# Moving work within a graph-and-expert kernel: loads, routing, one-hots and last steps in another order

## The chip, the cores and the metric

The kernel runs on one core of a Trainium2 chip. Its time is the device time of one execution in microseconds (us). The kernel before was run 9 times: median 2648.38 us, from 2645.98 to 2657.72. One execution was profiled.

## What is computed

A network of two layers over 3125 nodes with 256 features and 50000 edges, all in fp32. Each layer adds a graph convolution and a feed-forward part, each on a layer-normed input. The reference, cut (`seg_sum` and `seg_max` run over the edges of one target node `dst`):

```python
# layer 0: relational sums, 16 relations; then a mixture of 16 experts, 2 per node
h = layernorm(x)
x = x + seg_sum((h @ W_rel[r])[edge_type, src] * edge_weight, dst)
h = layernorm(x);  p = top2(softmax(h @ gate_w + gate_b))        # renormalized
x = x + sum_e p_e * ((silu(h @ w1[e]) * (h @ w2[e])) @ w3[e])
# layer 1: two graph attention convolutions of 8 heads; then shared MLP + 4 experts, 2 per node
def gat(h, W, a_src, a_dst, b):
    h = (h @ W).reshape(N, 8, 32)
    e = leaky_relu((h*a_src).sum(-1)[src] + (h*a_dst).sum(-1)[dst], 0.2)
    z = exp(e - seg_max(e, dst)[dst])
    return seg_sum(h[src] * (z / seg_sum(z, dst)[dst]), dst) + b
x = x + gat(elu(gat(layernorm(x), W1, ...)), W2, ...)
h = layernorm(x)
x = x + mlp3(h) + sum_e softmax(top2(softmax(h @ gW + gb)))_e * expert3_e(h)
```

The edges come sorted by target node.

## The kernel before

The nodes are cut into T = 25 tiles of R = 125. On PE, DVE, ACT and SP the instructions stand in the order in which the Python code issues them (`manual_schedule`), except for SP in the first stage, where a scheduler places the DMAs; POOL issues the indirect DMAs (gathers and scatters) in the code's order. Buffers come from pools with a fixed number of copies (`bufs`), so that a writer waits for the readers of the copy before. The stages follow one another:

**Table stage (0 to 604 us).** For each tile, in two halves of eight relations, PE multiplies the layer-normed rows by all relational weights `w_rel` (L1259, `p_tr`), ACT copies the product (L1262, `tr`, two copies) and SP writes it to a table in DRAM (L1266, 1 MB). Beside that the edges are read, sorted into records and placed (`edge_records` after tile 2, `places` from tile 3, `sent` after tile 6). From tile 11 on (SA) the first half of the relational sums runs along: POOL gathers table rows of the edges (L111), PE multiplies them by one-hot rows `hot` and adds (L987, `half_summed`). `weights(l)` (L1214) loads the matrix of attention layer l (`wx`) and its vectors (`av`), and multiplies them; it is called behind tiles 19 and 21.

**Second half of the sums, and routing (604 to 958 us).** The loop over the 25 `items` (one tile of sums each, 10 gathers on POOL) has in each pass: the two halves of an item's sums, `fetch` (gathers) for the item two ahead, `hot` for the next, `turn` (transposed rows) and `logits` (expert scores) for earlier items. The items are two batches, 11 (TA) and 14. When all logits of a batch are there, `routing` (L1400), a generator of steps of mainly DVE and some PE, ACT and SP work, chooses two experts per node, counts, and finds each row's position among the experts' slots; then it scatters the batch's rows to `xs` (L1509, two scatters per tile on POOL: 22 and 28). The expert slots of the first batch (19) and the second (22) are cut into a list of steps, `pieces`; `take(slot_steps, n)` issues the next n of them. `turn_slot` (L1545 to L1551) loads a slot's rows.

**Expert slots (to 1372 us).** The rest of the steps, PE-bound; `back_beside` for the first batch's way back runs beside them: gather each node's two expert rows, add them (`add_back`, L1617), layer-norm (`centred`, `factors`, L1372 to L1383), transpose, multiply by `wx1` (`first_hidden`, L1623) and write the rows of the first attention table (`h_tab`, L1626); `in_parts` (L929 to L933) splits the target scores into three bf16 parts `ad`. `back_alone` does the same for the second batch when nothing else is left (1372 to 1444 us).

**Attention layers (1444 to 1982 and 2021 to 2554 us) and end.** `layer` goes over the tiles; in pass s the tile `new` is s + 1, `now` is s, `old` is s - 1. Per tile POOL gathers 17 x 128 rows of 264 columns (256 features and 8 scores) into `g` in three PARTS (6, 6 and 5). `scans` (L1771) makes running maxima over the edges, `carried` (L1797) takes them across partitions, with PE's transposes `p_c`; `scores` (L1810) gives `z`, `weighted` (L1841) the products of rows and z into a tile `m`, `summed` (L1848) the sums by the one-hot `oh` on PE (L1852), `means` the division. `one_hot` (L1794) and `destinations` (L1790) for the next tile stand at the end of a pass. After a tile of layer 1 come elu and the product with `wx2` (`tail1` to `tail4`), written to the second table. Layer 2 has the last feed-forward beside it: the tiles go in 13 `pairs` (the last holds one tile) through the steps `normalize`, `first_layers`, `gates`, `second_layers`, `choice`, `shares`, `spread`, `shared_out`, `third_layers`, `finish` (out by L2151). `run` gives each step when its lag is reached: pair k is due in pass 2k + 2 + lag. Seven extra passes (`more`) drain them.

Of the kernel before, what the change touches and what calls it, by code (L numbers as in the profile page):

```python
# [7 lines left out]
F32 = mybir.dt.float32  # L8
# [35 lines left out]
def gnn_kernel(ctx: ExitStack, tc: tile.TileContext, a: dict, out: bass.AP):  # L44
# [834 lines left out]
    def by_tiles(ctx, start_i, hard):  # L879
# [124 lines left out]
        with ExitStack() as mk:  # L1004
# [5 lines left out]
            for r0 in range(0, RELS, 8):  # L1010
                for k in range(2):
                    nc.sync.dma_start(w_rel[:, k, r0:r0 + 8], a["L0_gnn_weight"]
                                      [r0:r0 + 8, k * 128:(k + 1) * 128, :].rearrange("r p o -> p r o"))
                if r0 == 0:
                    load_x(1, 5)
# [198 lines left out]
            def weights(l):  # L1214

                wx = keep.tile([128, 2, D + 2 * H], F32, name=f"wx{l}")
                nc.sync.dma_start(wx[:, :, :D], a[f"L1_gnn_W{l}"].rearrange("(k p) o -> p k o", p=128))
                av = sb.tile([128, 2, 2], F32, name="av", bufs=2)
                for k, name in enumerate((f"L1_gnn_a_src{l}", f"L1_gnn_a_dst{l}")):
                    nc.sync.dma_start(av[:, :, k], a[name].rearrange("h c -> (h c)")  # L1220
                                      .rearrange("(m p) -> p m", p=128), allow_slow_non_contiguous=True)
                ab = sb.tile([128, 2, 2, H], F32, name="ab", bufs=2)
# [52 lines left out]
            wx = []  # L1275
            with tc.manual_schedule():
# [3 lines left out]
                for t in range(T):  # L1280
# [29 lines left out]
                    if t == 2:  # L1310
# [12 lines left out]
                    elif t in (19, 21):  # L1323
                        wx.append(weights(len(wx) + 1))
# [4 lines left out]
            wx1, wx2 = wx  # L1329
# [3 lines left out]
        with ExitStack() as st:  # L1333
# [286 lines left out]
            def first_hidden(w):  # L1620
# [6 lines left out]
                in_parts(pool, ad1[:, w.t], h[:, DX:])  # L1627
# [24 lines left out]
            def back_alone(b):  # L1652
                for w in b.items[:3]:
                    fetch_back(w)
                for k in range(b.n + 2):
# [5 lines left out]
                    if 0 < k <= b.n:  # L1661
                        factors(b, k - 1, k)
                        turn(b.items[k - 1], wk_ps.tile([128, 512], F32, name="sum", bufs=2))
                    if k > 1:
                        first_hidden(b.items[k - 2])
# [11 lines left out]
            with tc.manual_schedule(engines={ET.PE, ET.DVE, ET.Activation, ET.SP}):  # L1677
                slot_steps = pieces()
                route, routed = routing(batches[0]), None
                for s, w in enumerate(items):  # L1680
                    if 1 <= s < 12:
                        k, c = (0, 4 * (s - 1)) if s < 6 else (1, 4 * (s - 6))
                        blank(k, c, min(c + 4, USED[k]))
                    for k in range(2):
                        summed(w.r, k)
                        if s + 2 < T:
# [3 lines left out]
                        if s > 1 and k == 0:  # L1690
                            logits(items[s - 2])
                        if s and k == 1:
                            turn(items[s - 1], w.r.p)
                        if s > TA and routed is None and not take(route, 8):
                            routed = s
                            take(slot_steps, 1)
                        if routed is not None and s > routed + 2:
                            take(slot_steps, 2)
                    summed_up(w.r)
                    centred(w)  # L1700
                    if routed is not None and s == routed + 2:
                        take(slot_steps, 11)
# [3 lines left out]
                take(slot_steps, 2)  # L1706
                logits(items[-1])
                route = routing(batches[1])
                while take(route, 1):
# [13 lines left out]
        with ExitStack() as st:  # L1723
# [28 lines left out]

            def fetch(w):
                w.g = []
                for k, (i0, i1) in enumerate(PARTS):
                    g = pool.tile([128, i1 - i0, DX], F32, name=f"g{k}", bufs=2)
                    for i in range(i0, i1):
                        gather(g[:, i - i0, :], w.h_tab, src_i[:, w.t, i:i + 1])  # L1760
# [49 lines left out]
            def scores(w):  # L1810
# [13 lines left out]
                w.m = [pool.tile([128, i1 - i0, DX], F32, name=f"m{k}") for k, (i0, i1) in enumerate(PARTS)]  # L1824
                for m, (i0, i1) in zip(w.m, PARTS):
                    nc.scalar.copy(m[:, :, D:], w.z[:, i0:i1])  # L1826
# [14 lines left out]
            def weighted(w, k):  # L1841
                i0, i1 = PARTS[k]
                m, g = (v[k][:, :, :D].rearrange("q i (h c) -> q i h c", h=H) for v in (w.m, w.g))
                nc.vector.tensor_mul(m, g, w.z[:, i0:i1, :, None].to_broadcast([128, i1 - i0, H, HD]))  # L1844

            def summed(w, k):
# [4 lines left out]
                for i in range(i0, i1):  # L1851
                    nc.tensor.matmul(w.p, w.oh[:, i, :], w.m[k][:, i - i0, :], start=(i == 0), stop=(i == CT - 1))  # L1852
# [12 lines left out]
            def layer(h_tab, ad, bias, tail1, tail2, tail3, tail4, slot=None, end=None, more=0):  # L1865
# [348 lines left out]
```

## Time and profile before

The profiled execution took 2648.1 us, its span 2646.3 us, at a mean granted TensorE clock of 0.856.

| engine | busy us | share of the span | instructions |
|---|---|---|---|
| PE (matmul) | 1995.1 | 75% | 8600 |
| PE weight load | 1447.2 | 55% | 8600 |
| DVE | 1353.9 | 51% | 2859 |
| ACT | 809.3 | 31% | 1701 |
| POOL | 1389.1 | 52% | 1445 |

By stage (busy us): table 0 to 604: PE 500, DVE 283, POOL 223. Sums and routing 604 to 958: PE 240, POOL 263. Slots 958 to 1372: PE 392. Way back 1372 to 1444: PE 36, DVE 36. Attention layer 1: PE 323, DVE 362, POOL 405 of 538. Layer 2: PE 408, DVE 398, POOL 403 of 533. End 2554 to 2646: PE 71.

In the chain that ended last PE has 43%, POOL 16%, issue 13%, DMA 13% and DVE 9%. The shares are averages over stages; "issue" is time in which an engine waited for nothing that the profile shows, and POOL's gathers each have 0.30 us of it in front.

### The profile page before, as it was taken

The page shows a single profiled execution, that of the slowest core. Times are in us where ns is not written, and L with a number is a line of the kernel's source. Part 1 is how long each engine was busy: PE and PEld are TensorE (multiplying, and loading weights), DVE is VectorE, ACT ScalarE, POOL GpSimd, SP SyncE. Part 2 cuts the span into 40 slices and gives each one's busy share as a digit, 9 for nine tenths or more (in the row PEclk, how much of TensorE's full clock was granted, in tenths as well). Part 3 has the DMA queues.
Part 4 walks back from the last instruction along what each step waited for, and adds up shares of the span by engine and source line. Part 5 has one row for each costly group of instructions (what it writes and reads, how often), then busy time and mean ns, then how long its engine had stood idle before and what let it go on. Part 6 is the DMA issues. An engine that isn't in the chain of part 4 may idle for free.

```text
span 2646.3 us, 26683 instructions
## 1 busy us (share of the span) xinstructions
PE 1995.1 (75%) x8600; PEld 1447.2 (55%) x8600; DVE 1353.9 (51%) x2859; ACT 809.3 (31%) x1701; POOL 1389.1 (52%) x1445
## 2 busy tenths in 40 slices
PE   6788998795655999998974366666653687888887
PEld 2334455454444888886862254444542465666665
DVE  1358673223351432132115476767763677888872
ACT  2222222120111232242223333333331354555542
POOL 0100677446777724120024777777773777777740
PEclk9789999897777999998985677777876788999998
DMA  6532555443345757664533655555552554454520
GB/s 216 196 118 112 182 178 193 143 142 107 105 128 184 220 168 246 206 208 130 195 107 92 156 140 140 139 140 139 141 154 52 136 136 133 137 148 133 150 72 19
DMA packets 191857, 386.35 MB, mean 146 GB/s; under 512 B 39698, under 2 KB 112386, under 8 KB 185957
## 3 DMA queue, kind: packets, MB, share of 16 engines
q0 software_dynamic: 76464, 189.38, 27.6%
q1 hardware_dynamic: 104091, 184.40, 20.5%
q10 hardware_dynamic: 11152, 10.75, 1.2%
q8 instruction: 71, 1.16, 0.2%
q14 instruction: 79, 0.65, 0.1%
HBM read 294.45 MB, written 89.87 MB: 145 GB/s over the span
## 4 chain that ended last, share of the span: by engine, by line
PE 43%; POOL 16%; issue 13%; DMA 13%; DVE 9%; ACT 3%; POOLq 1%; SPq 0%; DVEq 0%; ACTq 0%
POOL g L111 16%; PE ph L1559 10%; PE p_tr L1259 9%; DMA g<-h_tab_t,src_t 7%; PE p_sum L1852 6%; PE py L1569 5%; PE sum L987 5%; PE p_x L2049 2%; DMA table_t<-tr 1%; DVE m L1844 1%; PE p_x L2146 1%; DVE run L1799 1%; PE p_x L1737 1%; PE pt L1549 1%; DMA h_tab_t<-h 1%
## 5 line engine op out<-in xcount | busy, mean ns | idle before, releaser
L111 POOL DMA_INDIRECT g<-h_tab_t,src_t x850 | 808.1, 951 | 322.0 <-issue 268.2
L111 POOL DMA_INDIRECT g<-table_t,rg_t x450 | 440.3, 979 | 326.5 <-issue 244.2
L1852 PE MATMUL p_sum<-m,oh 128*125 128x264 f32 x1700 | 486.3, 449 | 28.0 <-DVE m L1844 28.0
L1852 PEld LDWEIGHTS p_sum<-m,oh 128*125 128x125 f32 x1700 | 372.0, 223 | 116.4 <-DVE m L1844 28.8
L1259 PE MATMUL p_tr<-w_rel_t,xT_t 128*125 128x512 f32 x800 | 381.0, 632 | 37.1 <-ACT tr L1262 34.9
L1559 PE MATMUL ph<-xcT,w 128*128 128x256 f32 x1312 | 310.5, 385 | 0.7 <-ACT xcT L1551 0.7
L987 PE MATMUL sum<-g,oh 128*125 128x256 f32 x900 | 240.3, 423 | 85.6 <-DMA g<-table_t,rg_t 66.2
L1259 PEld LDWEIGHTS p_tr<-w_rel_t,xT_t 128*125 128x125 f32 x800 | 157.5, 201 | 231.5 <-issue 181.1
L1559 PEld LDWEIGHTS ph<-xcT,w 128*128 128x128 f32 x1312 | 249.5, 193 | 33.9 <-ACT xcT L1551 1.1
L1563 DVE TENSOR_TENSOR hT<-silu,ph 128x256 f32<-128x256 f32 x164 | 69.0, 421 | 374.7 <-ACT silu L1562 374.6
L987 PEld LDWEIGHTS sum<-g,oh 128*125 128x125 f32 x900 | 185.9, 211 | 127.7 <-issue 79.7
L1844 DVE TENSOR_TENSOR m<-g,p_e 128x1536 f32<-128x1536 f32 x150 | 242.7, 1660 | 12.4 <-ACT m L1826 7.6
L1262 ACT COPY tr<-p_tr 125x512 f32<-125x512 f32 x200 | 114.6, 587 | 405.2 <-PE p_tr L1259 300.6
L111 POOL DMA_INDIRECT y<-ys,pos_i x50 | 61.5, 1229 | 323.1 <-DMA ys<-yc 217.4
L1569 PE MATMUL py<-w,hT 128*128 128x256 f32 x656 | 156.7, 382 | 0.2 <-DVE hT L1563 0.2
L1002 DVE TENSOR_TENSOR xr<-xr,sum 125x256 f32<-125x256 f32 x50 | 21.0, 419 | 250.1 <-PE sum L987 157.3
L1562 ACT ACTIVATE silu<-ph 128x256 f32<-128x256 f32 x164 | 62.8, 383 | 244.6 <-PE ph L1559 244.5
L1569 PEld LDWEIGHTS py<-w,hT 128*128 128x128 f32 x656 | 125.0, 192 | 17.1 <-DVE hT L1563 0.6
L1794 DVE TENSOR_TENSOR oh<-lo_t,fx 128x2125 f32<-128x2125 f32 x50 | 118.0, 2359 | 0.0
L1785 PE MATMUL p_c<-ident,fw 128*8 128x128 f32 x100 | 22.5, 313 | 120.9 <-DVE fw L1781 120.9
L1831 ACT ACTIVATE rows<-rows,minus_p 125x2176 bf16<-125x2176 bf16 x50 | 105.2, 2105 | 25.8 <-DMA g<-h_tab_t,src_t 17.3
L1832 ACT ACTIVATE ohT<-rows 125x2176 bf16<-125x2176 bf16 x50 | 100.7, 2016 | 1.6
(326 smaller groups left out, 2381.8 us busy)
## 6 DMA issues: line engine op xcount, KB each, us to landing
w<-in_L_ffn_w SPq DMA_DIRECT2D x123, 512.0 KB
table_t<-tr SPq DMA_DIRECT2D x46, 1000.0 KB
rows<-lo_rows_t SPq DMA_DIRECT2D x50, 531.2 KB
g<-h_tab_t,src_t POOLq DMA_INDIRECT x850, 2.9
xc<-xs_t SPq DMA_DIRECT2D x41, 256.0 KB
ys<-yc ACTq DMA_DIRECT2D x41, 256.0 KB
xs_t<-zero SPq DMA_DIRECT2D x9, 1024.0 KB
g<-table_t,rg_t POOLq DMA_INDIRECT x450, 5.3
```

Source lines behind the costliest of these rows:

```text
L111: return nc.gpsimd.indirect_dma_start(out=dst, out_offset=None, in_=table, in_offset=bass.IndirectOffsetOnAxis(ap=idx, axis=0))
L987: m = nc.tensor.matmul(r.p[:R, :D], r.oh[k][:, i - i0, :], r.g[k][:, i - i0, :], start=(i == r.parts[0][0]), stop=(i == r.parts[1][1] - 1))
L1259: m = nc.tensor.matmul(p, xT[:, k, t * R:(t + 1) * R], w_rel[:, k, r0:r0 + 2, :].rearrange("p r o -> p (r o)"), start=(k == 0), stop=(k == 1))
L1262: nc.scalar.copy(tr[:, 2 * q * D:(2 * q + 2) * D], p)
L1559: nc.tensor.matmul(p[:, which, :], u.w12[:, which, k, m * 128:(m + 1) * 128], u.xcT[:, k, :], start=(k == 0), stop=(k == 1))
L1563: nc.vector.tensor_mul(u.hT[:, m, :], s, p[:, 1, :])
L1569: nc.tensor.matmul(u.py[:, j, :], u.hT[:, m, j * 128:(j + 1) * 128], u.w3[:, m, :], start=(m == 0), stop=(m == nh - 1))
L1794: nc.vector.tensor_tensor(w.oh, lo[:, w.t, :, None].to_broadcast([128, CT, R]), iota_ps[:, None, :].to_broadcast([128, CT, R]), OP.is_equal)
L1831: nc.scalar.activation(w.rows, w.rows, AF.Abs, bias=minus_p[:R, :])
L1832: nc.scalar.activation(w.ohT.rearrange("r i q -> r (i q)"), w.rows, AF.Relu, bias=1.0, scale=-1.0)
L1844: nc.vector.tensor_mul(m, g, w.z[:, i0:i1, :, None].to_broadcast([128, i1 - i0, H, HD]))
L1852: nc.tensor.matmul(w.p, w.oh[:, i, :], w.m[k][:, i - i0, :], start=(i == 0), stop=(i == CT - 1))
```

## The change

- **w_rel** is loaded in 16 DMAs of two relations instead of 4 of eight, with `load_x(1, 5)` behind eight of them.
- **Attention weights**: `load_weights` issues the loads of both layers behind tile 1; `weights` still computes behind tiles 19 and 21.
- **Routing of the first batch** runs as a whole in pass 11, behind item 11's sums, with the turn of item 10 into a PSUM tile of its own; the fetch of item 13 stands behind it, and with it behind the scatters. Slot steps: 1 at the end of pass 11, 3 in pass 12, then 4 per pass (before: 1 in pass 12, 11 at the end of pass 14, then 4 per pass).
- **Routing of the second batch**: one slot step behind every second routing step instead of every one, and one step less ahead of it.
- **back_alone**: one copy per item instead of `in_parts`, and the parts for all 14 items in five operations at the end; the reciprocal stands one pass later than the root.
- **Attention layers**: `weighted` writes its product over the gathered rows; `g` has three copies, and `after_all` makes a part's first gather wait for the sums of the tile three before. `one_hot` and `destinations` of the tile `now` stand between its `scans` and `carried`. `weighted(now, 0)` stands before the means of the tile before; `tail4` one tile later.
- **Layer 2 and the end**: other lags; no extra passes; `last` issues the remaining steps of the last three pairs in a written order.

```diff
-            for r0 in range(0, RELS, 8):
+            for r0 in range(0, RELS, 2):
...
-                if r0 == 0:
+                if r0 == 6:
                     load_x(1, 5)
...
-            def weights(l):
+            def load_weights(l):
                 wx = keep.tile([128, 2, D + 2 * H], F32, name=f"wx{l}")
                 nc.sync.dma_start(wx[:, :, :D], ...)
...
+                return wx, av
+            def weights(wx, av):
...
+                    if t == 1:
+                        wx = [load_weights(l) for l in (1, 2)]
...
                     elif t in (19, 21):
-                        wx.append(weights(len(wx) + 1))
+                        weights(*wx[t // 20])
...
             def back_alone(b):
+                ad = pool.tile([R, b.n, H], F32, name="both")
...
                     if 0 < k <= b.n:
-                        factors(b, k - 1, k)
+                        v = b.sq[:, k - 1:k]
+                        nc.vector.tensor_scalar(v, v, 1.0 / D, EPS, op0=OP.mult, op1=OP.add)
+                        nc.scalar.activation(b.rstd[:, k - 1:k], v, AF.Sqrt)
...
                     if k > 1:
-                        first_hidden(b.items[k - 2])
+                        r = b.rstd[:, k - 2:k - 1]
+                        nc.vector.reciprocal(r, r)
+                        first_hidden(b.items[k - 2], ad)
...
                 for s, w in enumerate(items):
...
+                    if s == TA:
+                        logits(items[s - 2])
+                        turn(items[s - 1], ps.tile([128, 2, SL], F32, name="pt")...)
+                        logits(items[s - 1])
                     for k in range(2):
                         summed(w.r, k)
-                        if s + 2 < T:
+                        if s + 2 < T and s != TA:
                             fetch(items[s + 2].r, k, True)
...
-                        if s > TA and routed is None and not take(route, 8):
-                            routed = s
-                            take(slot_steps, 1)
-                        if routed is not None and s > routed + 2:
-                            take(slot_steps, 2)
+                        if s == TA:
+                            take(route, 8)
+                        elif s > TA:
+                            take(slot_steps, 2 if s > TA + 1 else 3 * k)
+                    if s == TA:
+                        while take(route, 1):
+                            pass
+                        for k in range(2):
+                            fetch(items[s + 2].r, k, True)
+                        take(slot_steps, 1)
...
-                    if routed is not None and s == routed + 2:
-                        take(slot_steps, 11)
...
-                take(slot_steps, 2)
+                take(slot_steps, 1)
                 logits(items[-1])
                 route = routing(batches[1])
-                while take(route, 1):
+                while take(route, 2):
                     take(slot_steps, 1)
...
-                    g = pool.tile([128, i1 - i0, DX], F32, name=f"g{k}", bufs=2)
+                    g = pool.tile([128, i1 - i0, DX], F32, name=f"g{k}", bufs=3)
...
+                    if len(added[k]) >= 3:
+                        after_all(rows[0], [added[k][-3]])
...
-                nc.vector.tensor_mul(m, g, w.z[:, i0:i1, :, None].to_broadcast(...))
+                nc.vector.tensor_mul(g, g, w.z[:, i0:i1, :, None].to_broadcast(...))
...
                     if now:
                         scans(now)
                     if new:
                         hot_rows(new)
+                    if now:
+                        one_hot(now)
+                        destinations(now)
+                    if older and s < T:
+                        tail4(older)
                     if now:
                         carried(now)
...
+                    if now:
+                        weighted(now, 0)
                     if old:
                         means(old)
                         tail1(old)
-                    if now:
-                        weighted(now, 0)
...
-                    if new:
-                        destinations(new)
-                        one_hot(new)
...
             def slot(s):
-                run(s, (1, first_layers), (2, second_layers), (4, spread), (6, third_layers))
+                run(s, (1, first_layers), (2, second_layers), (2, spread), (4, third_layers))
+            def mid(s):
+                run(s, (4, finish), (1, gates))
             def end(s):
-                run(s, (6, finish), (4, shared_out), (0, normalize), (1, gates), (2, choice), (3, shares))
+                run(s, (2, shared_out), (0, normalize), (1, choice), (1, shares))
+            def last():
+                u, v, w = pairs[-3:]
+                for step, p in ((third_layers, u), (finish, u), (first_layers, v), (normalize, w), (gates, v),
+                                (second_layers, v), (choice, v), (shares, v), (first_layers, w), (gates, w),
+                                (spread, v), (shared_out, v), (choice, w), (shares, w), (second_layers, w),
+                                (third_layers, v), (finish, v), (spread, w), (shared_out, w), (third_layers, w),
+                                (finish, w)):
+                    step(p)
```

## The prediction, written before the changed kernel ran

> **What bounds the kernel now.** I read the page's first three parts, then busy time by stage, the chain that ended last, the waits, and the order of work at each place that the diff touches. No engine bounds the whole: PE has 75% of the span and POOL 52%, but each stage has its own limit. The windows by stage (span; then busy time and count of PE, PEld, DVE, ACT, POOL; clock; DMA share; GB/s):
>
> ```profile
> 300.00:604.00 304.00, 270.36 (x990) 161.48 (x988) 134.24 (x219) 62.32 (x117) 183.62 (x182) 0.95 0.48 166
> 1444.00:1982.00 538.00, 323.41 (x1488) 238.54 (x1489) 362.07 (x707) 180.30 (x335) 405.22 (x426) 0.75 0.57 144
> 2021.00:2554.00 533.00, 407.96 (x2062) 310.81 (x2063) 398.13 (x878) 249.57 (x483) 403.20 (x425) 0.87 0.50 135
> 2554.00:2646.00 92.00, 71.22 (x293) 52.22 (x291) 34.68 (x123) 23.71 (x61) 0.00 (x0) 0.86 0.05 16
> ```
>
> To see: the table stage (to 604) is PE's. In the two attention layers no engine looks full, but POOL is: a gather is 0.951 busy and 0.30 of issue, 17 of them 21.25 a tile, and 25 tiles start 21.27 apart. 25 x 21.27 = 532 of each layer's 538 and 533. The last row is a tail without POOL, 92 us from the last gather's end.
>
> ```profile
> L111 POOL DMA_INDIRECT g<-h_tab_t,src_t x850 | 808.1, 951 | 322.0 <-issue 268.2
> L1794 DVE TENSOR_TENSOR oh<-lo_t,fx x50: 2358/2359/2362, 1463.6 to 2556.0; 128x2125 f32<-128x2125 f32 x50
> ```
>
> The sum is made against the profiled execution: 2648.1 us, span 2646.3; the runs' median is 2648.38, 0.3 above. Some 0.2%, 5.3 us, is what a measurement of this kernel can tell from no change.
>
> **Attention weights early: -24 (-27 to -19).** The chain (start, length, what):
>
> ```profile
> 454.97 13.61 DMA av<-in_L_gnn_a_src
> 473.06 8.38 PE p_tr L1259 x16
> ...
> 505.54 6.88 PE p_tr L1259 x16
> 514.31 13.42 DMA av<-in_L_gnn_a_dst
> 532.01 9.62 PE p_tr L1259 x16
> ```
>
> To see: after tiles 19 and 21 PE stands for the weights of an attention layer, whose load is issued only then, behind a 1 MB table write; the groups after it are slower than the usual 6.87. The sums' starts 453.39 to 481.28 and 512.24 to 541.47 are 27.89 and 29.23 apart where a half tile's period is 10.32: 17.57 + 18.91 = 36.5 us lost. The weights' own work, some 5.8 us a layer, stays: 36.5 - 2 x 5.8 = 24.9, less 1 for what may be left of the slow clock. The bounds are the two PE waits alone (11.49 + 11.27 = 22.8, less 4 if the computing is worse placed) and the sum plus 2.
>
> The loads now go out on SP behind the fourth table write, at tile 1, with tile 1's remaining writes and the edge loads queued behind. SP is slow there (an issue takes up to 8 us), so the edge chain (edge_records 75-97, places from 155) can slip. PE reaches that point only just in time (160.5): +1, from 0 to +5, the latter one such issue.
>
> **Relational weights in 16 loads: 0 (-2 to +5).** PE waited for the second pair of loads 0.37 and 1.83 us (at 19.67 and 22.60); that can go. Twelve more issues at the shortest seen for them, 0.418, are 5.0 if SP's own time decides; the bytes are the same, and PE is fed in order, so I take 0. The Trainium skill, "DMA: Bandwidth & Descriptors", Rules for kernel authors, speaks against it: batch to 1 MiB or more, and each load goes from 1 MB to 256 KB. Interpolated in that page's table the 4.2 MB would take an estimated 5 us longer; by it the sum would be 5 us less, by the 2.2 us row it is unchanged.
>
> **First routing behind the sums: -2 (-5 to +6).** It ran from 764.9 to 780.6 on DVE (15.7 us, 1.6 of it one item's hots in between), and its 22 scatters stood on POOL behind 20 more gathers, at 792.1 to 824.5; PE idled 31.19 us there for the first slot's rows. Now the routing stands alone behind item 11's sums, and the fetch of item 13 behind the scatters. POOL has no work of its own between: it reaches them at about 766.8 and the positions are ready at some 768.5, 2 us of stall. But the stage is POOL's: 250 gathers x 1.25 + 22 x 1.48 from 604.3 to 949.5 are the same instructions in another order, and the slot steps are the same 52 by the loop's end. The early slots fill PE's gap, which is not the limit: item time is 12.5 on POOL and 11.1 on PE. The loop's end (958.4) moves by the stall less slack in the last items. DVE and PE queue behind the routing; if its chain goes 8 us late, the stall is 8 and the sum +6. A gain of up to 5 is bounded by PE's lag behind POOL at the end, 958.4 - 949.5, about half of it.
>
> **Second routing: +6 (0 to +9).** Here the same idea takes work away. Before, a slot step stood between any two routing steps (15), now between every second (7), and one of four steps before it is gone:
>
> ```profile
> 977.89 3.62 PE L1559 MATMUL ph<-xcT,w 128*128 128x256 f32 x16
> 983.96 0.73 PE L1444 MATMUL sum<-both,before 125*125 125x224 f32 x2 [2.46 <-DVE both L1439]
> ```
>
> To see: with 15 steps interleaved, PE waited only 2.46 us for the routing's choice, at 25.6 us after the loop. Now that comes at about 23, as DVE has fewer slot products in between, but PE has only 9 steps, 15.4 us: idle 7.6, 5.1 more. Behind idle of 11 us the PE groups above took 1.5 to 2.8 longer than 6.87, so about 1 more. Scatters of this batch are first needed by slot 19, far later, so nothing comes back: 6. If the steps' ACT work covers it, 0; a choice 3 us later, 9.
>
> **Ends of batch 2's way back: -11 (-13 to -7).**
>
> ```profile
> 1405.32 0.68 PE L1389 MATMUL sum<-ident,xn 125*128 125x125 f32 x2 [1.82 <-ACT xT L1391]
> ...
> 1405.68 0.17 DVE L929 CAST ad<-h 125x8 bf16<-125x8 f32 x1 [0.48 <-ACT h L1625]
> ...
> 1406.49 0.17 DVE L933 CAST ad<-rest 125x8 bf16<-125x8 f32 x1
> 1406.58 1.00 DVE L1617 SCALAR_TENSOR_TENSOR xr<-y,wt,xr 125x256 f32<-125x256 f32 x2
> ...
> 1409.70 0.68 PE L1389 MATMUL sum<-ident,xn 125*128 125x125 f32 x2 [1.82 <-ACT xT L1391]
> ```
>
> To see: an item's period is 4.38 us (1405.32 to 1409.70), a loop of DVE and ACT in which five small parts of ad (5 x 0.2) stand before the next item's sum. One copy of 0.2 remains, and the reciprocal no longer waits for ACT's root: 4.38 - 0.81 = 3.57, x 14 = 11.3. The five batched operations at the end (14 x 8 elements, 0.2 to 0.35 each) lie beside the 24 us in which POOL waits for the last table write.
>
> **Attention layers.** Products in place, three row tiles: POOL's one wait for a product inside the layers, 3.33 at tile 2 of layer 1, goes: -3. Other tiles gain nothing, since POOL was never late. one_hot (2.36) and destinations (0.59) move from the end of an iteration to between scans and carried, ahead of the rest of the chain; there DVE waited for PE's first carry (63.8/50 = 1.3) and for the scans' ends, some 1.8, so a tile's latency grows by 1 to 2 but not its rate, at 14.2 (354/25) and 16.0 (399.5/25) of DVE busy per tile. Between layers the last sums (2000.66 to 2008.84), elu, and hs to the table (2017.61) set POOL's next start at 2021.48: the next layer's one-hot no longer delays elu by 2, the weighted product ahead of means by 2.45 does: +0.5 (-4 to +6).
>
> **The end without waits: -22 (-28 to -12).**
>
> ```profile
> 2578.85 7.76 PE p_sum L1852 x34
> 2587.55 5.35 PE p_x L2049 x24
> ...
> 2617.78 4.24 PE p_x L2146 x16
> 2629.21 7.69 PE p_x L2146 x16
> ```
>
> To see: after the last sums (2586.6) the steps of three pairs run one behind the other, with seven extra iterations of lags; out leaves at 2640.33, 53.7 later, 5.8 before the end. New lags put the third pair from the end ahead of the last sums, in waits that were there; those end at about 2581.5 (-5). Then, by their rows here: third layers of pair 10 3.5; first and gates of 11 7.9; second 3.1; choice 2.0; first of 12 5.8; spread and shared_out 2.9; choice of 12 and its exponent 3.2; third of 11 4.3; third of 12 and finish 4.4: 37.1, out at 2618.6 and the end at 2624.4. The slow row above, 7.69 against 4.24 for 16 matmuls, stands behind PE idle of 5.23; the Trainium skill, "TensorE: Matmul & The Clock Gate", Part 1, has the clock halve after an idle window of some 3.4 us. My chain's longest idle is 3.2; were the rule to bite there, the end would lose an estimated 3.4 of the gain, inside my bounds. The low end, -12, keeps half of the waits.
>
> **Sum.** -24 + 1 + 0 - 2 + 6 - 11 - 3 + 0.5 - 22 = -54.5: 2648.1 - 54.5 = 2593.6, say 2593.
>
> **Rivals.** (1) The ends don't shorten as worked out: tail -8 (the hand order waits for each softmax), way back -5 (ACT bounds its loop), second routing +9: 2593 + 14 + 6 + 3 = 2616. For: both are chains of short steps whose new order no trace shows. Against: the removed operations are seen in the loop. Chance 0.17.
> (2) Slower: the attention tile leaves POOL's pace. Place: DVE, from scans to weighted, where one_hot and destinations now stand. In layer 2 every second tile also has gates, choice and shares there: DVE busy 18.1 plus waits of 3 to 4 is 21.9 against 21.27. It decides from 21.27 a tile; each us over costs 50, and 1.1 over in both layers takes the 54.5. At 22.5: 61.5 more, 2655. For: it is close on odd tiles. Against: even tiles have 17, the third row tile averages the two, and layer 1 has 14.2. Chance 0.10.
> (3) POOL stands at the scatters for the routing: 10 us stall, 2603. For: nothing is left to hide it. Against: the chain is 15.7, 1.6 of it hots that now go elsewhere, and 12 of the other 14.1 fall beside gathers that are queued already. Chance 0.08, inside the range.
> (4) The weights' load at tile 1 delays the edge chain by as much as it saves: 2593 + 24 = 2617. Chance 0.05.
>
> **How the numbers follow.** My forecast, near 2593, has 0.60. The range 2574 to 2625 takes in the terms' ends half together and rivals 1, 3 and 4. Slower by over 0.2%: rival 2's 0.10. Within 0.2%: 0.03, out of rival 1, where a smaller overrun of the tiles joins it. Faster by over 0.2% (below 2643): the other 0.87.
>
> **What would show it.** Right: no PE wait for wx near tiles 19 and 21, p_tr at 6.87 throughout; periods of 21.27 on POOL in both layers, with no waits but issue; back items at 3.6; out issued 60 to 70 us after the last gather's end, against 86.5. Wrong: gathers of the attention layers waiting for p_sum, a POOL stall over 8 at the scatters, edge_records later than 100, or an end over 80 after the last gather.

## The result, and the profile after

The changed kernel took 2623.85 us (median of 10 runs, 2616.69 to 2633.66) against 2649.28 of the kernel before, now over 31 runs: 25.4 us less, a ratio of 0.9902 (95% interval 0.9889 to 0.9914). The prediction was 2593: direction right, the gain less than half of the 55 forecast. The time still lies inside the range of 2574 to 2625, just below its upper end. The profiled execution took 2618.6 us, its span 2616.9; stage by stage it is compared with the profile before (span 2646.3), so the stages add up to 29.4, not to the medians' 25.4.

Windows of the changed kernel at the stages that were shown before (span; busy time and count of PE, PEld, DVE, ACT, POOL; clock; DMA share; GB/s):

```profile
300.00:583.40 283.40, 268.01 (x990) 160.24 (x988) 135.06 (x221) 62.52 (x117) 183.92 (x182) 0.98 0.51 176
1417.00:1955.00 538.00, 301.15 (x1492) 227.02 (x1493) 362.45 (x704) 176.30 (x337) 406.08 (x426) 0.79 0.57 145
1993.00:2526.00 533.00, 405.32 (x2024) 308.82 (x2025) 390.95 (x865) 240.32 (x471) 403.21 (x425) 0.86 0.49 135
2526.00:2616.90 90.90, 70.89 (x330) 53.15 (x328) 44.83 (x137) 27.55 (x71) 0.00 (x0) 0.91 0.05 13
```

To see: the table stage is 21 us shorter at the same PE work and a clock of 0.98 instead of 0.95. The attention layers are as long as before. The tail behind the last gather, forecast to lose 22 of its 92 us, is 90.9 (91.1 from the gather's exact end).

Where the time went, from the starts and ends of the same instructions in both traces:

| stretch | forecast | measured | read from |
|---|---|---|---|
| table stage | -23 | -21.2 | end of the last p_tr, 593.2 to 572.0 |
| sums and first routing | -2 | -0.4 | end of the last sum, 958.5 to 936.9 |
| second routing and slots | +6 | +3.5 | last sum to first gather of batch 2's way back, 413.2 to 416.8 |
| batch 2's way back | -11 | -9.3 | that gather to the first attention gather, 72.8 to 63.5 |
| layer 1, tile 2 | -3 | -3.1 | 48.0 to 45.0 between the first gathers of tiles 0 and 2 |
| rest of the layers, with the way between them | +0.5 | +2.5 | to the end of layer 2's last gather, -30.4 to -28.0 in all |
| end | -22 | -1.5 | last gather's end to the span's end, 92.5 to 91.1 |

So one row of the table is far off. In the chain that ended last the end of the changed kernel reads, cut to its main pieces (start, length, what):

```profile
2533.93 5.34 PE p_x L2088 x24
2546.13 2.34 DVE oh L1826
2550.66 4.69 PE p_sum L1883 x10
2560.22 4.22 PE p_x L2185 x16
2564.45 7.76 PE p_sum L1883 x34
2572.21 4.04 PE p_x L2185 x16
2577.95 5.36 PE p_x L2088 x24
2601.27 5.34 PE p_x L2185 x16
```

To see: from the last sums' end (2572.2) out is issued at 2610.7, 38.5 us later, where it was 53.7 and 37.1 was forecast. The written order does what it should. But the sums themselves end 46.4 us behind the last gather's end (2525.85) instead of 32.8 before and 27.7 forecast. In front of them stands the one-hot of the last tile (2546.13), at a time when its rows had long been there. Three starts of DVE's scans and what it waited for between them, from two passes of layer 2 (timeline of DVE: start, length, operation, idle before):

```profile
2390.46 0.44 DVE L1813 TENSOR_TENSOR_SCAN fw<-cut_ft,es 128x136 f32<-128x136 bf16 x1 [1.48 <-ACT es L1810]
...
2399.65 1.75 DVE L1875 TENSOR_TENSOR g<-g,p_e 128x1536 f32<-128x1536 f32 x1 [0.78 <-DMA g<-h_tab_t,src_t]
...
2408.12 0.17 DVE L2099 TENSOR_REDUCE gm<-p_x 125x2 f32<-125x8 f32 x1 [1.11 <-PE p_x L2095]
...
2412.66 0.43 DVE L1813 TENSOR_TENSOR_SCAN fw<-cut_ft,es 128x136 f32<-128x136 bf16 x1
...
2431.94 0.69 DVE L2189 TENSOR_TENSOR xr<-xr,p_x 125x512 f32<-125x512 f32 x1 [2.70 <-PE p_x L2185]
...
2435.22 0.44 DVE L1813 TENSOR_TENSOR_SCAN fw<-cut_ft,es 128x136 f32<-128x136 bf16 x1 [1.48 <-ACT es L1810]
```

To see: two passes take 44.8 us, 22.4 each, and POOL gives a tile in 21.3 (over the whole layer a pass takes 22.0). DVE falls behind, and a third copy of the rows lets POOL go on. The first product waits for ACT (L1875, 0.78; the row names a DMA, but this tile's last gather had ended 23 us before, and ACT's copies of the exponent into the same tile end at 2399.62), gates and finish wait for PE (L2099, L2189), the scans for ACT behind normalize (L1813). Counted as "lag", the start of a tile's scans behind the end of its last gather:

| kernel | lag at tile 0, 8, 16, 24 of layer 2 | POOL's time a tile, layers 1, 2 | last gather to last sums | to out | last gather to end |
|---|---|---|---|---|---|
| before | 2.1, 2.3, 5.9, 5.8 | 21.44, 21.31 | 32.8 | 53.7 | 92.5 |
| changed | 2.2, 5.8, 13.5, 19.5 | 21.32, 21.31 | 46.4 | 38.5 | 91.1 |

The lag grows by 17 us over layer 2. At tile 24 it is 13.7 above that of before, and the last sums end 13.6 later behind the last gather: the lag is all of it. POOL, which the prediction watched, shows nothing.

### The profile page after: what moved, and what is told of

Same layout as the page of the kernel before. It is cut to its first block, busy times and chain, and to the rows that moved or that the text cites. A ratio compares the mean times of both kernels' runs of the same rounds, so it can differ in the third digit from the quotient of the medians.

```text
span 2616.9 us, 26717 instructions
## 1 busy us (share of the span) xinstructions
PE 1962.6 (75%) x8600; PEld 1428.6 (55%) x8600; DVE 1344.4 (51%) x2808; ACT 799.8 (31%) x1699; POOL 1389.4 (53%) x1445
## 3 DMA queue, kind: packets, MB, share of 16 engines
q0 software_dynamic: 76464, 189.38, 27.7%
## 4 chain that ended last, share of the span: by engine, by line
PE 29%; DVE 12%; POOL 8%; issue 6%; DMA 5%; ACT 4%; SPq 0%; ACTq 0%; POOLq 0%; DVEq 0%
PE ph L1563 8%; POOL g L111 8%; PE p_sum L1883 6%; PE py L1573 4%; DMA g<-h_tab_t,src_t 3%; PE p_x L2088 3%; DVE oh L1826 2%; DVE g L1875 2%; PE p_x L2185 2%; PE p_x L1765 1%; DMA xc<-xs_t 1%; DVE run L1831 1%; DMA h_tab_t<-h 1%; PE sum L1627 1%; PE pt L1553 1%
## 5 line engine op out<-in xcount | busy, mean ns | idle before, releaser
L1883 PE MATMUL p_sum<-g,oh 128*125 128x264 f32 x1700 | 468.6, 436 | 14.7 <-DVE g L1875 12.1
L1883 PEld LDWEIGHTS p_sum<-g,oh 128*125 128x125 f32 x1700 | 359.4, 215 | 97.3 <-DVE g L1875 12.5
L1262 PE MATMUL p_tr<-w_rel_t,xT_t 128*125 128x512 f32 x800 | 375.5, 624 | 45.0 <-ACT tr L1265 45.0
L1875 DVE TENSOR_TENSOR g<-g,p_e 128x1536 f32<-128x1536 f32 x150 | 245.0, 1662 | 46.3 <-ACT g L1857 32.2
L1956 PE MATMUL p_x<-ident,en 125*128 125x125 f32 x50 | 16.8, 437 | 142.1 <-DVE en L1985 142.1
L1855 ACT ACTIVATE p_e<-es 128x136 f32<-128x136 f32 x50 | 14.4, 287 | 318.4 <-DVE es L1853 318.4
```

What stands on the lines that cost most here:

```text
L1262: m = nc.tensor.matmul(p, xT[:, k, t * R:(t + 1) * R], w_rel[:, k, r0:r0 + 2, :].rearrange("p r o -> p (r o)"), start=(k == 0), stop=(k == 1))
L1875: nc.vector.tensor_mul(g, g, w.z[:, i0:i1, :, None].to_broadcast([128, i1 - i0, H, HD]))
L1883: m = nc.tensor.matmul(w.p, w.oh[:, i, :], w.g[k][:, i - i0, :], start=(i == 0), stop=(i == CT - 1))
```

## The experiments

The theory after the profile: **A**, layer 2's round on DVE, with its waits, is too long, because the one-hot was taken from the end of a pass, where it covered the waits for PE; the third row copy hides this from POOL and the end pays it. Rivals: **B**, the late last sums come from the order of the last tiles alone; **C**, the early first product makes the round long. Later **D** and **E** ask what the new lags and the written order do. (The expectations put a tile's landing 2.9 us behind its last gather's end, and their 0.1 and 17.4 are the one-hot's starts counted from there; in the profile before a gather landed 2.9 us after its issue, 1.9 after its end. The growth of 17 is the same.) Runs with the same letter were made in one job on one chip, with the kernel before beside them.

**e1, one-hot of layer 2 back at the end of a pass**

```diff
                     if now:
-                        one_hot(now)
+                        if not slot or s == 0:
+                            one_hot(now)
                         destinations(now)
...
+                    if slot and now and new:
+                        one_hot(new)
                     if mid and now:
                         mid(s)
```

> In the profile of the changed kernel the scans of layer 2 start later after their rows have landed from tile to tile: 0.1 us at tile 0, 17.4 at tile 24, so a pass takes about 22.1 us where POOL gives rows every 21.27; the end pays it. Theory A: the round of DVE with its waits is too long, since the one-hot (2.34) was taken from the end of a pass, where it covered the waits for PE (finish 8.38 and gates 4.21 us per 8 tiles), and put where only the carry's wait is. Put back there in layer 2, it covers some 12 per 8 tiles and uncovers about 5: pass at most 21.3, lag at tile 24 under 6, end after the last gather 78 to 81 instead of 91, time about 2612. Rival B (the late last sums come from the last two tiles' own order and not from a lag that grows): lag and time unchanged, 2620 to 2628. Rival C (the weighted product ahead of the means makes the round long): lag at tile 24 still over 12, 2620.

**e2, first product of layer 2 behind means and residual**

```diff
-                    if now:
+                    if now and not slot:
                         weighted(now, 0)
                     if old:
                         means(old)
                         tail1(old)
+                    if now and slot:
+                        weighted(now, 0)
+                    if old:
                         tail2(old)
```

> In layer 2 the first product stands behind the means and the residual of the tile before, as in the kernel before; all else as changed. It waited 7.2 us per 8 tiles for the exponent on ACT. Rival C: these 0.9 us per tile are what the round is too long by: pass 21.3, lag at tile 24 under 6, time about 2613. Theory A (the one-hot's place): a part of the wait goes, but the finish and gates waits stay and the sums start 2 us later on PE, which finish waits for: pass 21.6 to 22, lag at tile 24 8 to 15, time 2616 to 2623. Rival B: unchanged, 2620 to 2628.

**e3, normalize ahead of finish**

```diff
-                run(s, (4, finish), (1, gates))
+                run(s, (0, normalize), (4, finish), (1, gates))
...
-                run(s, (2, shared_out), (0, normalize), (1, choice), (1, shares))
+                run(s, (2, shared_out), (1, choice), (1, shares))
```

> In even passes of layer 2 normalize stands ahead of finish, so that its three DVE steps and ACT's root and products run while DVE would wait for the third layers on PE, and the copies for the next scans come earlier on ACT. The waits of finish and of the scans are 14.3 us per 8 tiles in the changed kernel. If the round sets the end (theory A, C), some 5 of them go, 0.6 a tile: lag at tile 24 about 6 to 9, time about 2614. Rival B: unchanged, 2620 to 2628.

**e4, the three together**

> One-hot at the end of the pass, first product behind the means, normalize ahead of finish, all in layer 2. If the round is the cause, the pass cannot become shorter than POOL's 21.27, so the three together give little more than the best of them: lag at tile 24 at most 4, end after the last gather 76 to 80, time 2608 to 2612. If the lag does not depend on the round (rival B), 2620 to 2628.

These four ran on a chip on which the kernel before took 3172.07 us. They took 3317.58, 3321.05, 3315.57 and 3311.73, ratios of 1.0463, 1.0468, 1.0457 and 1.0447 (intervals of +-0.005). One of ACT's waits in e1 there, and the same in the same kernel on the next chip (f1); engine, tile and line, what it waited for, then us in total, times, longest:

```profile
ACT xT L1993 <- remote: 247.8, 22, 12.1
```

```profile
ACT xT L1993 <- PE p_x L1959: 30.5, 25, 1.2
```

To see: ACT waits up to 12 us for transposes for which it waits 1.2 elsewhere; the update that ends these waits comes long after the transposes' own records, most often about 3 us after the end of POOL's last gather. Such stalls stand in all stages from 600 us on and POOL's tile takes 30 to 36 us, so these runs tell nothing of A, B and C. They do warn that the sign of the change need not hold on every chip: four kernels that differ from it in one to three places, and are faster than before elsewhere, lose 4.5% there. The changed kernel itself was not run there, and what holds the updates back stays open.

**f1 to f4, the same four kernels again, on another chip**

> One-hot of layer 2 back at the end of a pass, all else as changed. In the profile of the changed kernel the scans of layer 2 start later after their rows have landed from tile to tile: 0.1 us at tile 0, 17.4 at tile 24; a pass takes about 22.1 us where POOL gives rows every 21.27, and the end pays it. Theory A (the one-hot was taken from where it covered the waits for PE, finish 8.38 and gates 4.21 us per 8 tiles): pass at most 21.3, lag at tile 24 under 6, time 0.983 to 0.988 of before. Rival B (the late last sums come from the last tiles' own order, not from a lag that grows): unchanged, 0.990. Rival C (the product ahead of the means makes the round long): lag still over 12, 0.989. A first run of this kernel, on a chip where the kernel before took 3172 us, gave 1.046: stalls of 10 to 33 us between PE and ACT stood in all stages there; where those are, no theory on the lag can be told.

> First product of layer 2 behind the means and the residual of the tile before, all else as changed. It waited 7.2 us per 8 tiles for the exponent. Rival C: pass 21.3, lag at tile 24 under 6, 0.985. Theory A: the finish and gates waits stay, pass 21.6 to 22, lag 8 to 15, 0.986 to 0.990. Rival B: 0.990.

> Normalize ahead of finish in even passes of layer 2, all else as changed. Theory A and C: of the waits of finish and the scans, 14.3 us per 8 tiles, some 5 go: lag at tile 24 about 6 to 9, 0.986. Rival B: 0.990.

> The three edits together, in layer 2 only. If the round sets the end, a pass cannot fall below POOL's 21.27, so they give little more than the best alone: lag at tile 24 at most 4, end after the last gather 76 to 80 instead of 91, 0.982 to 0.985 of before. Rival B: 0.990.

The kernel before took 2649.64 us here.

| kernel | median us | ratio (95%) | lag at tile 0, 8, 16, 24 | last gather to last sums | last gather to end |
|---|---|---|---|---|---|
| f1, one-hot | 2606.74 | 0.9840 (0.9813 to 0.9867) | 2.2, 7.1, 8.1, 7.8 | 32.5 | 77.1 |
| f2, product | 2613.87 | 0.9866 (0.9836 to 0.9896) | 2.2, 5.8, 6.0, 12.2 | 38.9 | 83.5 |
| f3, normalize | 2609.81 | 0.9849 (0.9823 to 0.9876) | 2.3, 4.6, 5.1, 5.0 | 30.7 | 77.9 |
| f4, all three | 2605.54 | 0.9829 (0.9799 to 0.9858) | 2.2, 2.3, 6.1, 2.2 | 25.9 | 70.5 |

To see: in f1 the last order is untouched, and the tail is 14 us shorter than the changed kernel's 91.1, as is the time to the last sums. Rival B falls: edits in the middle of a pass, 24 times over, move the end. f1's time is where A put it. Its lag of 7.8 is above the 6 expected, but it comes in one step at tile 7 (from 2.2 to 7.0) and grows no further.

Eight passes of layer 2, from the scans of tile 14 to those of tile 22, in the kernel before, the changed kernel and f1 (columns as in the windows above; the third busy time is DVE's):

```profile
2347.00:2517.10 170.10, 145.43 (x753) 111.31 (x752) 138.61 (x317) 87.56 (x173) 128.68 (x137) 0.94 0.50 141
2325.80:2501.60 175.80, 147.69 (x754) 113.41 (x753) 138.66 (x317) 86.43 (x173) 132.98 (x141) 0.92 0.49 140
2321.00:2491.90 170.90, 144.78 (x752) 110.83 (x752) 139.38 (x317) 86.25 (x173) 129.46 (x137) 0.94 0.48 141
```

What DVE waited for in these passes, the lines on the carries (`run`), finish (`xr`) and the gates (`gm`); us in total, times, longest. In the kernel before:

```profile
DVE run L1799 <- PE p_c L1786: 9.2, 8, 2.1
```

in the changed kernel:

```profile
DVE xr L2189 <- PE p_x L2185: 8.4, 4, 2.7
DVE gm L2099 <- PE p_x L2095: 3.1, 3, 1.1
```

in f1:

```profile
DVE run L1831 <- PE p_c L1818: 5.0, 4, 1.4
DVE xr L2192 <- PE p_x L2188: 0.9, 2, 0.5
```

and in f2, where the product no longer waits but the division in front of it does:

```profile
DVE rd L1889 <- PE p_sum L1883: 7.7, 8, 1.6
```

To see: DVE's work is the same in all three kernels, 17.3 to 17.4 us a pass; only its waits differ, 3.9 a pass before, 4.6 in the changed kernel, 3.9 again in f1. The moved one-hot covers the wait for the carries (`p_c`), which was 9.2, and uncovers finish and gates, which had no wait of that kind before; f1 trades them back: 7.5 and 3.1 less, 5.0 more, 5.6 in eight passes, which is the whole 0.7 a pass. That is theory A's mechanism. Against the kernel before the other waits grew too (4.0 us in eight passes, for the product, the scans and the gates' exponents), so the one-hot is not the only cause of the longer round. PE's granted clock was 0.92 in the changed kernel's passes and 0.94 in the others; whether that adds to the waits or follows from them is not separated.

The one-hot's place is not the only remedy, though: f3 leaves it where the change put it, and its lag stays at 5.1 or below, its tail 13 us shorter. f2 came out as A expected of it (lag 8 to 15, 0.986 to 0.990), and C falls: from tile 16 to 24 its lag grows by 6.2, as the changed kernel's does by 6.0, and its tail of 83.5 is not clear of the 86.5 and 87.2 of g2 and g4 below, which leave layer 2 as changed. So the round is too long by 0.7 us a pass, and putting the one-hot back or normalize ahead takes that much away. The three edits together give little over the best alone: once the round keeps POOL's pace there is no growing lag left to remove.

**g1, lags and extra passes of before in layer 2, without the written order.** Edit: `slot`, `end`, the loop's range and `more=7` as before the change, `mid` and `last` gone.

> The changed kernel with the lags and the seven extra passes of before in layer 2, without the written last order; one-hot, in-place products and three row tiles stay. In the profile of the changed kernel out is issued 38.5 us after the last sums, before 53.7. Theory D (the written order is worth these 15 and the lags do not make the round long): lag at tile 24 still 12 to 18, last sums to out 52 to 55, time 2636 to 2642. Theory E (the shorter lags, with finish right behind its third layers, make the round long): lag under 6, last sums to out 53, time 2625 to 2630.

2630.85 us (ratio 0.9913, 0.9882 to 0.9944; before 2652.53 in this job). Last sums to out: 54.0, so the written order, with the lags that leave room for it, is worth 15, as D said. But the lag at tile 24 is 11.3, below the 12 of D and above the 6 of E, against 15 to 21 in the four profiles that have the change's layer 2 unaltered (the changed kernel, g2, g3, g4). D and E are both half right: the new lags and the written order save 15 behind the last sums and add some 4 to 9 to the lag.

**g2, second routing with one slot step per step**

```diff
-                take(slot_steps, 1)
+                take(slot_steps, 2)
                 logits(items[-1])
                 route = routing(batches[1])
-                while take(route, 2):
+                while take(route, 1):
                     take(slot_steps, 1)
```

> Second routing as before: one slot step behind each routing step and two ahead; all else as changed. From the end of the sums to the first gather of the way back the changed kernel took 416.8 us, the one before 413.2. If the thinner interleave costs this (the prediction's term of 6, measured 3.5): 413 to 414 and 2620. If the same work only comes later elsewhere: 416 to 417, 2624.

2619.11 us (0.9879, 0.9841 to 0.9918). PE at the second routing, in the changed kernel and in g2:

```profile
958.82 1.11 PE L1448 MATMUL sum<-both,before 125*125 125x224 f32 x2 [6.31 <-DVE both L1443]
```

```profile
961.38 0.64 PE L1448 MATMUL sum<-both,before 125*125 125x224 f32 x2 [2.45 <-DVE both L1443]
```

To see: with the steps put back PE waits 3.9 us less. From the last sum to the way back's first gather g2 took 417.3, the three others of its job 420.8 to 421.4. The changed kernel's profile had 416.8 on another chip, which is why the expectation's 413 was missed; within the job the thinner interleave costs 3.5 to 4 us, as much as PE waits longer. Over all jobs but that of e1 to e4 it costs more: nine profiles with the thin interleave took 416.8 to 421.7 us, five with the dense one 411.0 to 417.3 (the kernel before, g2, h1, h3, h4), and the means, 420.3 and 413.8, are 6.5 apart.

**g3, attention weights loaded late** (each layer's `load_weights` called behind tiles 19 and 21, where its `weights` is)

> Loads of the attention weights issued behind tiles 19 and 21 again; all else as changed. If the early issue alone gave the 21.2 us of the table stage: p_tr ends at 593, time about 2645. If the load competes with table writes wherever it stands, less than 10 is lost: 2630.

2645.27 us (0.9965, 0.9947 to 0.9984); the last p_tr ends at 592.3 instead of 572.0. The early issue alone gives 20 of the table stage's 21 us.

**g4, batch 2's way back as before** (`first_hidden` and `back_alone` of before)

> The second batch's way back as before (five parts per item, factors in one step); all else as changed. If those operations were the period: 72.8 from the first gather of the way back to the first attention gather instead of 63.5, time about 2633. If the period is set by ACT: under 5 lost, 2628.

2635.26 us (0.9934, 0.9913 to 0.9955); 73.2 us from the first gather of the way back to the first attention gather. Within the job, 2635.26 - 2619.11 is 16, of which g2's routing is 4 and its shorter tail (86.5) 1; in its own stretch the edit is worth 9.7.

**h1, best of these**: the three edits of e4 and g2's routing. **h4**: the same with e2's move in both layers.

> The three edits of layer 2 (one-hot at the end of the pass, first product behind the means, normalize ahead of finish) and the second routing with one slot step per step, all else as changed. The lag stays under 4 at tile 24 and the PE wait in the second routing falls from 6.3 to 2.5: 0.9815 of before, 2600 to 2603 where before is 2650. If the routing's gain is given back in the slots: 0.983.

> As the best kernel, with the first product behind the means in layer 1 too. The way from layer 1 to layer 2 (last gather's start to next first gather's) was 41.97 in the changed kernel and 40.37 before; the early product was put down for 2.45 of it. If so: 39 to 40, time 2 below the best. If ACT's elu and the sums set it: 41.5 to 42.5, time unchanged.

h1 took 2600.63 us (0.9824, 0.9806 to 0.9842), h4 2594.09 (0.9803, 0.9775 to 0.9831), against 2649.83 before. From the last gather's start of layer 1 to the first of layer 2 it took 45.1 in h1, 38.4 in h4, 42.0 in the changed kernel and 40.4 before. h1 and h4 differ in layer 1's first product alone, and the nine other kernels with it early, three row copies and no stalls took 41.9 to 44.8: early, it costs 3.5 to 7 us there. The times of h1 and h4 themselves are not clear of each other. The tail is 73.3 in h4. h4 beats both kernels, and comes to where the prediction had put the change, with the routing's thinner interleave, the one-hot's move in layer 2 and the early product undone and normalize put ahead of finish.

**h2, two copies of the gathered rows**

```diff
-                    g = pool.tile([128, i1 - i0, DX], F32, name=f"g{k}", bufs=3)
+                    g = pool.tile([128, i1 - i0, DX], F32, name=f"g{k}", bufs=2)
...
-                    if len(added[k]) >= 3:
-                        after_all(rows[0], [added[k][-3]])
+                    if len(added[k]) >= 2:
+                        after_all(rows[0], [added[k][-2]])
```

> The changed kernel with two copies of the gathered rows instead of three. If the third copy hides the long round from POOL (rows are now held until their sums are done, some 54 us from a tile's first gather): POOL waits for p_sum at every tile, a tile takes about 27 us instead of 21.27 in both layers, 2850 to 2920. If the third copy is not needed: 2624.

2684.27 us (1.0130, 1.0111 to 1.0149). What POOL waited for:

```profile
POOL g L111 <- PE p_sum L1883: 65.4, 41, 9.7
```

To see: the wait that the third copy hid. POOL's tile takes 23.6 us in layer 1 and 22.6 in layer 2, the lag in layer 2 is 2.2 at tiles 0, 8, 16 and 24, and the tail is 74.0, 17 below the changed kernel's. The expectation's 27 us a tile was too much, perhaps because each third of the rows comes free on its own. So the copy is needed, and without it the cost of layer 2 stands on POOL and not at the end. Not all of that cost is the long round: layer 1, which keeps POOL's pace with three copies, loses as much, since rows are held until their sums are done.

**h3, the kernel before with one_hot and destinations between scans and carried, and nothing else**

> The kernel before with one_hot and destinations between scans and carried, and nothing else changed. Theory A as the whole cause: with the products in tiles of their own and two row copies the long round shows on POOL: waits for the products at most tiles of layer 2, 0.5 to 0.9 us a tile, time 2658 to 2672. If the move makes the round long only together with the new lags and the early product: POOL at 21.27, time 2645 to 2655.

2653.81 us, ratio 1.0010 (0.9995 to 1.0026): no difference that can be told from none. In its profile POOL's tile in layer 2 is 21.56 instead of 21.31 and the lag at tile 24 is 6.1. The move alone costs some 6 us over the layer on POOL, not the 17 of lag. With g1 (11.3 at tile 24 under the old lags) that leaves the move together with other edits, the new lags among them; their shares are not separated.

## Why the prediction was right in six terms and wrong in one

- **Attention weights: right.** Forecast -24 and +1, measured -21.2 in the stretch, and g3 gives back 20.
- **Relational weights: right.** PE started tile 1 at 26.8 instead of 30.5, but tile 11 at 258.1 instead of 257.7: nothing stays. The estimate of 5 us more that the table of the Trainium skill's page ("DMA: Bandwidth & Descriptors", Bandwidth) would give for the smaller loads is not seen; the trace disagrees with it here: PE's first tile no longer waits for a load, where it had waited 0.37 and 1.83 us.
- **First routing: right in its stall,** 2.01 us at POOL's scatters, forecast 2. Of the gain of 2 the stretch shows 0.4.
- **Second routing: right.** PE waits 6.31 us (7.6 were forecast), 3.9 more than with the dense interleave. The stretch lost 3.5 in the first pair of profiles and 6.5 in the mean of all, forecast 6; the part beyond PE's wait is not traced.
- **Way back: right.** The period came out as worked out, in the changed kernel:

```profile
1379.56 0.68 PE L1393 MATMUL sum<-ident,xn 125*128 125x125 f32 x2 [1.00 <-ACT xT L1395]
...
1383.13 0.68 PE L1393 MATMUL sum<-ident,xn 125*128 125x125 f32 x2 [1.01 <-ACT xT L1395]
```

  3.57 us an item, as forecast; the stretch became 9.3 us shorter, 11.3 were forecast.
- **The wait at tile 2 of layer 1: right.** 3.1 of 3 went.
- **The end: wrong, and the step that failed stands in the paragraph on the attention layers.** There the tile's latency was to grow "but not its rate, at 14.2 and 16.0 of DVE busy per tile". That compares busy time with POOL's 21.27 and leaves out DVE's waits; and 16.0 is a mean over the whole layer, when the later passes had 17.3. Over the eight passes shown DVE of the kernel before was busy 17.3 us a pass and waited 3.9: 21.3, just POOL's pace. In the changed kernel it was busy 17.3 and waited 4.6: 22.0. The prediction saw only the wait that the moved one-hot covers (p_c's), not those that it uncovers (finish and gates), and it gave the new lags no price at all for DVE's round.
- **The tail's term** took the last sums to end 27.7 us behind the last gather. In f4, h1 and h4, where the lag is gone or small, they end at 25.9, 27.0 and 28.9: the number was that of a pass that keeps POOL's pace. From the sums on the forecast held: 37.1 to out, measured 38.5.
- **Rival 2 had the mechanism and the wrong price.** It named DVE from scans to weighted and said 21.9 for an odd tile, but weighed it against an even tile of 17 without waits, and paid for it on POOL, 50 us for each us over. With three row copies POOL does not pay. What is paid is the lag of the last tile, 24 passes x 0.7 us, at the end, which is the very place from which the gain of 22 was to come. The check that the prediction named for it (gathers waiting for p_sum) shows nothing in such a kernel; the one that caught it was "an end over 80 after the last gather", with out at 84.8 against the 60 to 70 forecast.
- **The time inside the range is luck.** The upper end of 2625 was set for the terms' ends half together and for rivals 1, 3 and 4. The weights' load delayed nothing (4), POOL did not stand at the scatters (3), and the tail, the only end that failed to shorten, failed by the lag and not by the order that rival 1 doubted.

## What to carry to other kernels

Where a producer runs ahead through several buffers, compare its period with the consumer's whole round, waits included, and look at how the consumer's lag grows over the loop; a wait on the producer appears only when the buffers are full, and until then the cost is paid at the end. An operation without dependencies that fills a wait is worth its place: before moving it, list the wait that it covers now. A third buffer can be needed for an in-place product and still turn a visible stall into a hidden one.

## What the runs showed of the hardware

The clock fell in the tail without a long idle. After a wait of 1.67 us that ended at 2589.56, PE in the changed kernel was never idle for more than 0.63 us until 2597, with short groups between; yet (windows; the number after POOL's is the granted clock):

```profile
2589.00:2593.00 4.00, 3.30 (x24) 2.90 (x24) 0.77 (x7) 2.17 (x7) 0.00 (x0) 1.00 0.02 4
2593.00:2597.00 4.00, 3.23 (x19) 2.19 (x18) 1.13 (x5) 0.94 (x4) 0.00 (x0) 1.00 0.00 0
2597.00:2601.00 4.00, 1.92 (x8) 1.63 (x9) 2.83 (x20) 0.71 (x3) 0.00 (x0) 0.51 0.00 0
```

The longer wait of 2.08 us (to 2600.06) came when the clock had already fallen. The third layers behind it (2601.27) took 5.34 us, where those of 2560.22 took 4.22. The Trainium skill, "TensorE: Matmul & The Clock Gate", Part 1, speaks of an idle window of some 3.4 us before the clock halves; here the clock halved after 8 us of which PE was busy for 6.5, with no idle longer than 0.63. What made it fall stays open.

And the chip, or something else that came with one job, matters more than the change: the kernel before took 2648 to 2653 us in four jobs and 3172 in one. In that one ACT started up to 33 us after the last record of what it needed from PE, and kernels that took 0.983 to 0.987 of before elsewhere took 1.045 to 1.047 of it. Each job ran on a chip of its own, so chip and job cannot be told apart.
